# Keys of a pair copied by ScalarE alone, and one exponential moved behind a copy, in a multi-query attention kernel

## The chip, the cores and the metric

The kernel runs on one core of one Trainium2 chip. The metric is the device time of one execution in microseconds (us); the median of several runs is compared. Engines are named as the profile names them: PE is TensorE's matmuls and PEld its weight loads, DVE is VectorE, ACT is ScalarE, POOL is GpSimdE, SP is the engine that issues most DMAs.

## The reference

Multi-query attention with a residual over 64 batches of 128 tokens, width 512, 16 heads of 64; all heads share one set of keys and values. A null key and value, the first two rows of `cond`, stand ahead of the keys. Cut to what matters:

```python
xn = layernorm(x, g_in)
q = (xn @ Wq).reshape(b, n, H, DH).transpose(0, 2, 1, 3) * scale
kv = xn @ Wkv
k, v = (kv[..., :DH], kv[..., DH:])
k = jnp.concatenate([nk, k], axis=1); v = jnp.concatenate([nv, v], axis=1)
sim = jnp.einsum('bhid,bjd->bhij', q, k) + bias      # bias, causal mask, key mask
attn = jax.nn.softmax(sim, axis=-1)
out = jnp.einsum('bhij,bjd->bhid', attn, v)
out = out.transpose(0, 2, 1, 3).reshape(b, n, INNER) @ Wo
return x + layernorm(out, g_out)
```

The kernel subtracts the null key and the null value from all keys and values as they leave PSUM, so that the null column needs no matmul; the null value is added back to the attention's result.

## The kernel before

Batches are worked on in 32 pairs, and x is loaded and transposed in groups of four batches (two pairs). The program's order is written out by hand: each engine carries out its instructions in the order in which the code names them, and waits at an instruction whose operands are not ready. Pair d passes through `turn(d)` and then `body(d)`; `body_first` stands for pair 0, and `turn_end`, `body_end` and `body_last` for the last two pairs. So `body` runs 29 times, for d = 1 to 29.

A turn makes the scores of pair d on PE, adds the bias (DVE), takes maxima of the first half (DVE), takes the exponentials of the first half of the pair's first batch (`exps(a, 0)`, eight on ACT), multiplies the weights of the pair before by the values (PE, line 781, tile `po`) and has ACT add the null value and copy them out (line 800, tile `oT`).

A body then does four things at once for different pairs, interleaved by hand:

- Keys and values of the pair after next. `kv_pair` is eight matmuls (line 363) into the PSUM tile `pkv`: keys in partitions 0 to 63, values in 64 to 127. `kv_pair_out` copies them out: DVE takes the values (line 380, tile `vT`, 64x256), then the first two of the four blocks of 32 tokens of the keys (line 389, tile `kT`, 64x128), and ACT takes the other two blocks, one at a time (line 393, 64x64 each). In odd bodies `values_T` follows on DVE (line 401, tile `vb`), since then a group's values are complete. A DMA on SP doubles the keys (line 396).
- Queries of the pair after next, as the seven products of a Strassen scheme: `product(g, f, k, ...)` (line 515) is four matmuls of 256 columns. Products 1, 6, 7 and 4 add up in one PSUM tile `pa`, and between them `keep` (line 527) has ACT copy the intermediate sum to SBUF: `kp` after product 1, `ku` after product 6 and again after product 7. Product 7 adds to `pa` and so has to wait until the `ku` copy of product 6 has read it. Between product 6 and product 7, PE has product 5 into another tile, `pc` (four matmuls).
- The output projection of the pair before (`out_product`, line 868; tiles `pyX`, `pyY`, `pyw`) in the same scheme; `kyp` (line 882) is ACT's copy of its product 1. Its layer norm is two pairs late: statistics and the negated scaled mean `nmro` on DVE (line 919), the normalisation `yn` on ACT (line 926).
- The rest of the softmax: `exps(b, hf, lo, hi)` (line 683) is one ACT exponential per head row with an accumulated sum, `rinv` (line 701) on DVE, `scale` (line 705) on POOL, `blocks_T` (line 721) on DVE.

In an even body POOL also makes sums of tokens for the next group (`xS`, line 497), of which product 7 uses the third. GpSimd's power for the reciprocal root is line 281, tile `rstd`.

The exponentials of the pair's second batch, `exps(b, 0, ...)`, are dealt out between the copies: four ahead of `kyp` and the first `ku`, two behind them, `yn`, then the last two, then the `ku` of product 7.

Of the kernel before, what the change touches and what calls it, by code (L numbers as in the profile page):

```python
# [10 lines left out]
AF = mybir.ActivationFunctionType  # L11
ALU = mybir.AluOpType
# [5 lines left out]
def kernel(  # L18
# [59 lines left out]
    nc = tc.nc  # L78
# [19 lines left out]
    PLACE = 0, 1, 3, 2  # L98
# [47 lines left out]
    nkv = const.tile([P, 1], FP, name="nkv")  # L146
    nkv_neg = const.tile([P, 1], FP, name="nkv_neg")
# [201 lines left out]
    K_ROWS, V_ROWS = slice(0, DH), slice(DH, P)  # L349
# [25 lines left out]
    def kv_pair_out(m, pkv):  # L375
        g, t = divmod(m, GB)
        if t == 0:
            vTs[g] = hp.tile([P, GB, N], FP, tag="kv", name=f"vT_{g}", bufs=1)
        two = slice(t, t + 2)
        nc.vector.tensor_scalar(  # L380
            vTs[g][V_ROWS, two],
            pkv[V_ROWS].rearrange("p (t n) -> p t n", t=2),
            nkv[V_ROWS],
            None,
            ALU.subtract,
        )
        src = pkv[K_ROWS].rearrange("p (t i q) -> p t i q", t=2, i=NQ)
        out = kT[K_ROWS, :, two].rearrange("p i t q -> p t i q")
        nc.vector.tensor_scalar(
            out[:, :, 0:2], src[:, :, 0:2], nkv[K_ROWS], None, ALU.subtract  # L390
        )
        for i in (2, 3):
            nc.scalar.activation(
                out[:, :, i], src[:, :, PLACE[i]], AF.Identity, bias=nkv_neg[K_ROWS]
            )
        nc.sync.dma_start(out=kT[V_ROWS, :, two], in_=kT[K_ROWS, :, two])

# [280 lines left out]
    def exps(b, hf, lo=0, hi=R8):  # L678
        if hf == 0 and lo == 0:
            rsum[b] = small.tile([P, 2, R8], FP, tag="rsum", name=f"rsum_{b}")  # L680
        for k in range(lo, hi):
            row = S[b][:, k, WITH_NULL[hf]]
            nc.scalar.activation(  # L683
                row,
                row,
                AF.Exp,
                bias=nmax[b][:, hf, k : k + 1],
                accum_out=rsum[b][:, hf, k : k + 1],
            )
# [335 lines left out]
    def body_first():  # L1025
# [11 lines left out]
        for f in range(2):  # L1037
            product(g, f, 1, *rooms_a[f])
            keep_of(f, "p1")
        kv_pair_out(g * GB, pkv)  # L1040
        norm_apply(m)
        for f in range(2):
# [202 lines left out]
    def body(d):  # L1245

        a, b, p, l = 2 * d, 2 * d + 1, 2 * d - 2, 2 * d - 4
        g, h = d // 2 + 1, d % 2
        q, soft = g < NG, d > 0
        out, ln = 0 <= p <= P_LAST, 0 <= l <= P_LAST  # L1250
# [20 lines left out]
        if q:  # L1271
            kv_pair_out(g * GB + 2 * h, pkv)
            if h == 1:
                values_T(g)
# [28 lines left out]
            pair_residual(l)  # L1303
            store(l)
        if soft:
            exps(b, 0, 0, 4)
        if out:
            out_sum(p, 0)
        if sums:
# [7 lines left out]
            product(g, f0, 6, ps_q, "a", start=False)  # L1317
            keep("a", "u2")
        if soft:
            exps(b, 0, 4, 6)  # L1320
        if ln:
            pair_norm(l + 1, (ps_y, "Y"))
        if q:
# [166 lines left out]
    norm_stats(6)  # L1490
    null_negative()
    kv_pair_out(0, pkv)
    norm_stats(7)
    causal(1)
# [81 lines left out]
    for d in range(1, PAIRS - 2):  # L1576
        turn(d)
        body(d)
# [42 lines left out]
```

## Time and profile before

| what | value |
|---|---|
| median of 3 runs | 1035.4 us (1035.14 to 1035.87) |
| the profiled execution's own time | 1035.41 us |
| its span, first to last instruction | 1033.6 us |
| PE / PEld busy | 1021.9 us (99%) / 895.9 us (87%) |
| DVE / ACT / POOL busy | 805.6 / 689.1 / 744.8 us |
| granted TensorE clock, mean | 1.000 |

Times in the views are microseconds from the span's start. A row of the timeline gives start, length, engine, line, operation and tiles, the count of merged instructions, and in brackets the engine's idle time ahead and what ended it. A row of the waits gives who waited for whom, the total, how often, and the longest. The chain of work that ended last shows piece by piece (start, length, engine, tile, line) what each step was released by; "issue" in it is time without a wait that the profile shows. Buffer numbers are left out of names in the profile (`ku`, `pa`).

### The profile page before, as it was taken

What the parts mean: (1) busy time and instruction counts of PE and PEld (TensorE: products, weight loads), DVE (VectorE), ACT (ScalarE), POOL (GpSimd) and SP (SyncE); (2) the same over time, 40 slices, a digit from 0 to 9 for tenths busy, and PEclk for the clock granted to TensorE, in tenths of its full rate; (3) what the DMA queues carried; (4) which work ended last, traced back from release to release, by engine and by line L of the source; (5) the groups of instructions that cost most, each with busy time, mean ns of one, the idle gap of its engine ahead of it and who ended that gap; (6) DMA issues with size and microseconds to landing.
All of it is one profiled execution on the core that took longest, in us unless ns stands there. A gap on an engine that the chain in (4) does not pass through costs nothing.

```text
span 1033.6 us, 31331 instructions
## 1 busy us (share of the span) xinstructions
PE 1021.9 (99%) x12345; PEld 895.9 (87%) x12345; DVE 805.6 (78%) x1806; ACT 689.1 (67%) x2773; POOL 744.8 (72%) x579
## 2 busy tenths in 40 slices
PE   9999999999999999999999999999999999999997
PEld 8888888888888888888888888888888888888886
DVE  6877777877778877788777788777887777877697
ACT  4766667666677666686656776666776667856582
POOL 4997768686685857758677686766868678586676
PEclk9999999999999999999999999999999999999999
DMA  6414152141522315233152421415223151230211
GB/s 212 141 56 127 65 153 82 54 129 63 164 75 91 99 60 165 68 107 113 44 151 68 132 98 49 139 62 158 81 71 109 63 170 69 92 88 28 82 64 62
DMA packets 73835, 100.86 MB, mean 98 GB/s; under 512 B 32212, under 2 KB 36056, under 8 KB 71896
## 3 DMA queue, kind: packets, MB, share of 16 engines
q1 hardware_dynamic: 73392, 98.47, 31.0%
q8 instruction: 96, 1.57, 0.7%
q14 instruction: 51, 0.42, 0.1%
q10 hardware_dynamic: 296, 0.40, 0.1%
HBM read 63.19 MB, written 33.55 MB: 94 GB/s over the span
## 4 chain that ended last, share of the span: by engine, by line
PE 90%; ACT 4%; DVE 3%; issue 1%; POOL 1%; DMA 0%; POOLq 0%; DVEq 0%; ACTq 0%
PE pa L515 18%; PE pyX L868 17%; PE pyY L868 10%; PE pc L515 9%; PE po L781 7%; PE pkv L363 6%; PE pyw L868 5%; PE pl L581 4%; PE pq L450 3%; PE ps L652 3%; PE sc_X L652 2%; ACT s L683 2%; PE sc_Y L652 2%; PE py_s L868 1%; PE sc_a L652 1%
## 5 line engine op out<-in xcount | busy, mean ns | idle before, releaser
L683 ACT ACTIVATE s<-s,nmax 128x65 f32<-128x65 f32 (+1 forms) x1024 | 372.7, 368 | 62.5 <-DVE nmax L674 62.5
L705 POOL TENSOR_TENSOR s<-s,rinv 128x512 f32<-128x512 f32 (+1 forms) x132 | 190.6, 1445 | 152.2 <-DVE rinv L701 152.2
L617 POOL TENSOR_TENSOR s<-biasp,mneg 128x1552 f32<-128x1552 f32 (+1 forms) x65 | 206.1, 3173 | 51.1 <-DVE s L667 38.2
L683 ACT ACTIVATION_READ_ACCUMULATOR s<-s,nmax 128x1 f32 x1024 | 196.2, 192 | 0.0
L515 PE MATMUL pa<-xS,wq 128*128 128x256 f32 x472 | 123.8, 385 | 2.3 <-ACT ku L527 2.3
L533 ACT COPY qT<-pa 128x256 f32<-128x256 f32 x59 | 22.0, 372 | 153.5 <-PE pa L515 153.5
L674 DVE TENSOR_REDUCE nmax<-s 128x8 f32<-128x1032 f32 (+1 forms) x128 | 121.7, 951 | 0.1
L721 DVE STREAM_TRANSPOSE sb<-s 128x1536 f32<-128x1536 f32 (+1 forms) x68 | 113.5, 1672 | 2.0 <-POOL s L705 2.0
L868 PE MATMUL pyX<-wT,oT 128*128 128x256 f32 x464 | 109.7, 379 | 0.0
L868 PE MATMUL pyX<-wo,oT 128*128 128x256 f32 x464 | 109.7, 379 | 0.0
L515 PEld LDWEIGHTS pa<-xS,wq 128*128 128x128 f32 x472 | 85.1, 190 | 21.6 <-ACT ku L527 7.9
L868 PEld LDWEIGHTS pyX<-wo,oT 128*128 128x128 f32 x464 | 86.0, 190 | 10.5
L868 PEld LDWEIGHTS pyX<-wT,oT 128*128 128x128 f32 x464 | 85.9, 190 | 10.7
L848 POOL TENSOR_TENSOR oT<-oT 128x512 f32<-128x512 f32 x64 | 80.4, 1274 | 4.3 <-PE pyw L868 2.1
L781 PE MATMUL po<-sb,vr 32*64 32x256 f32 (+1 forms) x4064 | 81.0, 300 | 0.0
L781 PEld LDWEIGHTS po<-sb,vr 32*64 32x64 f32 x4064 | 70.9, 130 | 8.1 <-issue 5.7
L281 POOL TENSOR_TENSOR rstd<-rstd,nhalf 128x1 f32<-128x1 f32 x64 | 35.1, 555 | 57.0 <-DVE rstd L280 54.5
L536 DVE TENSOR_TENSOR qT<-pc,ku 128x256 f32<-128x256 f32 x118 | 48.5, 411 | 33.1 <-PE pc L515 18.9
L597 DVE TENSOR_TENSOR qT<-pl,kp 128x128 f32<-128x128 f32 x112 | 31.1, 277 | 55.5 <-PE pl L581 53.8
L800 ACT ACTIVATE oT<-po,nv 128x512 f32<-128x512 f32 (+1 forms) x127 | 73.7, 654 | 0.1
L363 PE MATMUL pkv<-xT,wkv 128*128 128x256 f32 x256 | 63.3, 391 | 0.0
L515 PE MATMUL pc<-xS,wS 128*128 128x256 f32 x236 | 60.6, 379 | 0.0
(187 smaller groups left out, 2402.6 us busy)
## 6 DMA issues: line engine op xcount, KB each, us to landing
res<-in_x_dram SPq DMA_DIRECT2D x64, 256.0 KB
x<-in_x_dram SPq DMA_DIRECT2D x63, 256.0 KB
out_dram<-y SPq DMA_DIRECT2D x63, 256.0 KB
xd<-xb SPq DMA_DIRECT2D x14, 1024.0 KB
xT<-xd SPq DMA_DIRECT2D x56, 256.0 KB
vr<-vd SPq DMA_DIRECT2D x64, 128.0 KB
kT<-kT SPq DMA_DIRECT2D x32, 64.0 KB
vd<-vb SPq DMA_DIRECT2D x32, 64.0 KB
```

Of the source, the lines that this page charges most:

```text
L363: nc.tensor.matmul(pkv, wkv[:, kc, :], xT[g][:, t : t + 2, kc, :], start=(kc == 0), stop=(kc == KC - 1),)
L515: nc.tensor.matmul(prod[tag], w[:, kc, f * P : (f + 1) * P], t[:, :, kc, :], start=(start and kc == 0), stop=(kc == HK - 1), skip_group_ch ...
L617: nc.gpsimd.tensor_tensor(S[b][:, :, keys], biasp[:, :, keys], mneg[:, t, keys] .unsqueeze(1) .broadcast_to([P, R8, keys.stop - keys.start ...
L652: nc.tensor.matmul(home[r][u * DH : (u + 1) * DH, f, :], qT[g, f, t // 2][rows, t % 2, hf, u], kT[rows, 0 : nk // Q, t, :], start=True, st ...
L674: nc.vector.tensor_reduce(nmax[b][:, hf], S[b][:, :, WITH_NULL[hf]], AX.X, ALU.max, negate=True)
L683: nc.scalar.activation(row, row, AF.Exp, bias=nmax[b][:, hf, k : k + 1], accum_out=rsum[b][:, hf, k : k + 1],)
L705: nc.gpsimd.tensor_tensor(sv, sv, rinvs[b, hf][:, lo:hi].unsqueeze(2).broadcast_to([P, hi - lo, sv.shape[2]]), ALU.mult,)
L721: nc.vector.transpose(sbs[b][:, :, lo:hi].rearrange("p j e q -> p e j q"), S[b][:, lo:hi, 1 : ROW - 1].rearrange("p e (j k) -> p e j k", k=Q),
L781: nc.tensor.matmul(po[s][rows, to : to + n], vr[g][quad, t, PLACE[j], :], sb[quad, slots, r * NF : (r + 1) * NF, :], start=(turn == 0), st ...
L800: nc.scalar.activation(to, src, AF.Identity, bias=nv2)
L848: eng.tensor_tensor(o, a, b, op)
L868: nc.tensor.matmul(prod[key], h[:, c, :], w[:, c, :], start=(start and c == 0), stop=(c == HC - 1), skip_group_check=not start,)
```

## The change

`kv_pair_out` no longer has DVE copy the first two key blocks; ACT copies all four, in three instructions (two blocks together, then one and one). DVE keeps the values alone. In `body`, the fourth exponential of `exps(b, 0, ...)` moves from ahead of `kyp` and the first `ku` to behind them.

```diff
@@ kv_pair_out
         src = pkv[K_ROWS].rearrange("p (t i q) -> p t i q", t=2, i=NQ)
         out = kT[K_ROWS, :, two].rearrange("p i t q -> p t i q")
-        nc.vector.tensor_scalar(
-            out[:, :, 0:2], src[:, :, 0:2], nkv[K_ROWS], None, ALU.subtract
-        )
-        for i in (2, 3):
+        for at, to, n in ((0, 0, 2), (3, 2, 1), (2, 3, 1)):
             nc.scalar.activation(
-                out[:, :, i], src[:, :, PLACE[i]], AF.Identity, bias=nkv_neg[K_ROWS]
+                out[:, :, to : to + n],
+                src[:, :, at : at + n],
+                AF.Identity,
+                bias=nkv_neg[K_ROWS],
             )
         nc.sync.dma_start(out=kT[V_ROWS, :, two], in_=kT[K_ROWS, :, two])
@@ body
         if soft:
-            exps(b, 0, 0, 4)
+            exps(b, 0, 0, 3)
@@ body
             product(g, f0, 6, ps_q, "a", start=False)
             keep("a", "u2")
         if soft:
-            exps(b, 0, 4, 6)
+            exps(b, 0, 3, 6)
```

The rows below are the built program's order, without times; rows with - stand before, rows with + after the change. On DVE, in the body of pair 3 (`pkv_1758` is its keys and values, `vT_1375` the group's values, `nmro` the negated means of the two late batches):

```order
 L908 TENSOR_SCALAR rstdo_1772<-mvo_1770 128x1
 L380 TENSOR_SCALAR vT_1375<-pkv_1758,nkv 64x256
-L389 TENSOR_SCALAR kT<-pkv_1758,nkv 64x2x2x32
 L401 STREAM_TRANSPOSE vb_1780<-vT_1375 64x512
 L919 TENSOR_SCALAR nmro_1790<-mvo_1567,rstdo_1569 128x1
```

The key copy is gone from DVE, and the transpose of the values and the two `nmro` follow the values' copy directly. On ACT, at the same place, from the last two copies of the attention's result (`oT`) to the first normalisation (`yn`):

```order
 L800 ACTIVATE oT_1749<-po_2_1670,nv_88 128x2x8x32
 L800 ACTIVATE oT_1749<-po_3_1671,nv_88 128x2x8x32
-L393 ACTIVATE kT<-pkv_1758,nkv_neg 64x64 x2
+L390 ACTIVATE kT<-pkv_1758,nkv_neg 64x2x2x32
+L390 ACTIVATE kT<-pkv_1758,nkv_neg 64x64 x2
 L527 COPY kp_1812<-pa_2_1_1809 128x256
 L926 ACTIVATE yn_1814<-y_1464,nmro_1790,rstdo_1569 128x512
```

ACT has one more instruction of 64 partitions by 128 elements ahead of the two that it had. On ACT, directly behind that (`s_1555` is the scores of the pair's second batch; the - and + rows of `kyp` and `ku` differ by buffer numbers alone):

```order
-L683 ACTIVATE s_1555,rsum_1827<-s_1555,nmax_1763 128x65 x4
-L882 COPY kyp_1839<-pyX_1_1834 128x256
-L527 COPY ku_1845<-pa_2_1_1809 128x256
-L683 ACTIVATE s_1555,rsum_1827<-s_1555,nmax_1763 128x65 x2
+L683 ACTIVATE s_1555,rsum_1827<-s_1555,nmax_1763 128x65 x3
+L882 COPY kyp_1838<-pyX_1_1833 128x256
+L527 COPY ku_1844<-pa_2_1_1809 128x256
+L683 ACTIVATE s_1555,rsum_1827<-s_1555,nmax_1763 128x65 x3
 L926 ACTIVATE yn_1849<-y_1576,nmro_1792,rstdo_1772 128x512
```

One exponential of the four ahead of `kyp` and `ku` now stands behind them. PE, POOL and SP have the same instructions in the same order as before.

## The prediction

> **What bounds the kernel now.** I read the page's first section, then who waits on PE and PEld, then one body of each parity row by row, then the chain through the odd one.
>
> ```profile
> PE 1021.9 (99%) x12345; PEld 895.9 (87%) x12345; DVE 805.6 (78%) x1806; ACT 689.1 (67%) x2773; POOL 744.8 (72%) x579
> ```
>
> PE is busy for 99% of the span; no other engine is above 78%. So the time is PE's, and the change, which leaves PE's instructions alone, can only pay where PE stands waiting. By the waits of the weight loads and, last row, of the matmuls:
>
> ```profile
> PEld pa L515 <- ACT ku L527: 7.9, 14, 0.6
> PEld pa L515 <- POOL rstd L281: 3.9, 13, 0.3
> PEld pa L515 <- POOL yS L848: 0.3, 1, 0.3
> ```
>
> ```profile
> PE pa L515 <- ACT ku L527: 2.3, 14, 0.2
> ```
>
> 14 times a load for `pa` waits 0.56 us for ACT's `ku`, and 13 + 1 times 0.3 us. I looked at where these stand: the first kind once in each odd body from 3 to 29, the second once in each even body from 2 to 28, always ahead of product 7 of the body's first column pair. Here are products 6, 5, 7 and the next PE work, first in an odd body, then in the even one behind it:
>
> ```profile
> 448.81 1.03 PE L515 MATMUL pa<-xS,wS 128*128 128x256 f32 x4
> 449.67 1.03 PE L515 MATMUL pc<-xS,wS 128*128 128x256 f32 x4
> 450.86 1.13 PE L515 MATMUL pa<-xS,wq 128*128 128x256 f32 x4 [0.16 <-ACT ku L527]
> 451.83 1.89 PE L868 MATMUL pyw<-wo,oT 128*128 128x256 f32 x8
> ```
>
> ```profile
> 480.46 1.03 PE L515 MATMUL pa<-xS,wS 128*128 128x256 f32 x4
> 481.33 1.03 PE L515 MATMUL pc<-xS,wS 128*128 128x256 f32 x4
> 482.27 1.10 PE L515 MATMUL pa<-xS,wq 128*128 128x256 f32 x4
> 483.21 1.03 PE L868 MATMUL pyw<-wo,oT 128*128 128x256 f32 x4
> ```
>
> Unhindered, four such matmuls take 0.86 us from start to start (448.81 to 449.67), so products 5 and 7 together should take 1.73. They take 451.83 - 449.67 = 2.16 in the odd body and 483.21 - 481.33 = 1.88 in the even one: **0.43 and 0.15 us lost**. The row shows 0.16 of idle only, since the modelled end of product 5 hides the rest. The weight loads give the same delay another way:
>
> ```profile
> 449.46 0.84 PEld L515 LDWEIGHTS pc<-xS,wS 128*128 128x128 f32 x4
> 450.86 0.73 PEld L515 LDWEIGHTS pa<-xS,wq 128*128 128x128 f32 x4 [0.56 <-ACT ku L527]
> ```
>
> ```profile
> 481.11 0.84 PEld L515 LDWEIGHTS pc<-xS,wS 128*128 128x128 f32 x4
> 482.24 0.73 PEld L515 LDWEIGHTS pa<-xS,wq 128*128 128x128 f32 x4 [0.29 <-POOL rstd L281]
> ```
>
> Product 7's first load should come 0.86 behind product 5's, at 450.32 and 481.97. It is 0.54 and 0.27 late and costs 0.43 and 0.15. So the first **0.11 us of lateness are free**, twice the same figure.
>
> What makes it late in the odd body is the chain that ended last:
>
> ```profile
> 446.20 0.04 DVE vT L380
> ...
> 446.72 0.35 DVE kT L389
> ...
> 447.09 0.71 DVE vb L401
> ...
> 447.83 0.23 DVE nmro L919
> ...
> 448.14 0.78 ACT yn L926
> 448.92 1.36 ACT s L683 x8
> 450.29 0.26 ACT kyp L882
> 450.54 0.28 ACT ku L527
> ...
> 450.86 1.13 PE pa L515 x4
> ```
>
> It runs through both things that the change touches: DVE's key copy (0.35 us) delays `nmro`, which delays `yn`; behind `yn` stand four exponentials (1.36 us with their accumulator reads), `kyp` and `ku`.
>
> **The change part by part.** *DVE loses line 389.* The values' copy ends at about 446.70; the next DVE row starts at 446.72 instead of 447.09, so `vb`, `nmro` and, if ACT is ready, `yn` come 0.35 earlier: `yn` at 447.79.
>
> *ACT gains one copy.* Rows needed:
>
> ```profile
> 447.15 0.51 ACT L393 ACTIVATE kT<-pkv,nkv_neg 64x64 f32<-64x64 f32 x2 [0.40 <-DVE kT L389]
> 447.56 0.36 ACT L527 COPY kp<-pa 128x256 f32<-128x256 f32 x1
> ...
> 450.44 0.36 ACT L527 COPY ku<-pa 128x256 f32<-128x256 f32 x1
> ```
>
> ```profile
> 478.80 0.51 ACT L393 ACTIVATE kT<-pkv,nkv_neg 64x64 f32<-64x64 f32 x2 [0.39 <-PE pa L515]
> ...
> 481.76 0.37 ACT L527 COPY ku<-pa 128x256 f32<-128x256 f32 x1
> ```
>
> ```profile
> L800 ACT ACTIVATE oT<-po,nv 128x512 f32<-128x512 f32 x116 | 69.2, 672 | 0.0
> ...
> L393 ACT ACTIVATE kT<-pkv,nkv_neg 64x64 f32<-64x64 f32 x64 | 16.3, 302 | 17.0 <-DVE kT L389 10.9 <-PE pa L515 6.1
> ```
>
> Both groups are the same function with a bias column, read from PSUM: 302 ns for 64 elements, 672 for 512. A straight line gives 355 ns for 128. Two 64-wide ones move the queue on by 447.56 - 447.15 = 0.41, 0.205 each, so neighbours overlap by 0.10, and the new copy moves it on by **0.26 us**. Bounds: 0.20 (the 64-wide one) and 0.57 (the 512-wide one). I take 0.26, near the lower end, as the row of 64 is the nearer one. [...]
>
> In the built program the first key copy waits for DVE's values' copy (446.70) where it waited for DVE's key copy (447.07). The hand-over took 0.08 (447.07 to 447.15), so ACT starts at 446.79 instead of 447.15, 0.36 earlier, and ends its key work at 446.79 + 0.26 + 0.41 = 447.46; `kp` takes 0.26 of queue, and ACT could start `yn` at 447.72. `nmro` allows 447.79. So the added copy is hidden behind `nmro`, with 0.07 to spare.
>
> *One exponential moves.* A quarter of 1.36 is 0.34. So `yn` 447.79, exponentials 448.57 to 449.59, `kyp` to 449.84, and `ku` could start there: 0.35 + 0.34 earlier. But now something else is late: product 6 itself.
>
> ```profile
> 462.67 1.03 PE L515 MATMUL pa<-xS,wq 128*128 128x256 f32 x4
> ```
>
> ```profile
> 463.78 0.37 ACT L527 COPY ku<-pa 128x256 f32<-128x256 f32 x1 [0.74 <-PE pa L515]
> ```
>
> An ACT that stands ready starts its copy 0.08 after the product's modelled end (463.70 to 463.78). Product 6 ends at 448.81 + 1.03 = 449.84, so `ku` starts at 449.92, ends at 450.28, and the load follows 0.06 later as before (450.80 to 450.86): 450.34, 0.02 late, within the free 0.11. **The 0.43 goes wholly.**
>
> *Even body.* ACT starts its keys 0.36 earlier (478.44), has 0.26 more to do (-0.10 from there on), and one exponential less (-0.34): `ku` could start at 481.32. Product 6 ends at 480.46 + 1.03 = 481.49, so `ku` starts at 481.57 and ends at 481.94; with 0.11 to the load as before (482.13 to 482.24), 482.05, 0.08 late: free. **The 0.15 goes too.** This takes the load there to wait for `ku`, whose end is 0.11 ahead of it, rather than for POOL's `rstd`, which product 7 does not read.
>
> *What is behind.* The moved exponential puts off the `ku` of product 7 by 0.34. In the odd body ACT reaches the first `ku` 0.52 earlier (449.92 for 450.44), so it is still ahead; in the even one only 0.19 earlier (481.57 for 481.76), so the second comes 0.15 later than here:
>
> ```profile
> 484.07 0.37 ACT L527 COPY ku<-pa 128x256 f32<-128x256 f32 x1
> ```
>
> ```profile
> 485.50 0.73 PEld L515 LDWEIGHTS pa<-xS,wq 128*128 128x128 f32 x4
> ```
>
> Product 4's load, which needs that copy, comes 1.06 behind its end now, and would still come 0.76 behind with the copy at 484.59 and the load 0.15 earlier. The keys' DMA leaves about when it did, and its keys are read two turns later. The one place where PE, now earlier, may meet DVE is product 5 of the odd body's second column pair, whose tile is free when DVE has read it:
>
> ```profile
> 456.45 0.42 DVE L536 TENSOR_TENSOR qT<-pc,ku 128x256 f32<-128x256 f32 x1
> ```
>
> ```profile
> 456.93 0.73 PEld L515 LDWEIGHTS pc<-xS,wS 128*128 128x128 f32 x4
> ```
>
> DVE works without a pause from `vT` to there and ends at 456.87, just 0.06 ahead of the load. DVE gains 0.35, PE 0.43, so the load comes 0.08 late. That is under 0.11: I cost it at nothing, and if the margin is missing there it costs up to 0.08 x 14 = 1.1 us.
>
> **Sum**, against the profiled execution (1035.41 us, span 1033.6): 14 x 0.43 + 14 x 0.15 = 6.0 + 2.1 = 8.1 us. 1035.4 - 8.1 = 1027.3; the median of the runs shown is the same 1035.4. Body 1 has no such wait, and the start and the last pairs I cost at nothing (PE has no wait on a key copy there).
>
> **The rivals.**
> - *Given back in the same body*, by DVE as above or by a like margin: 1.1 us, so 1028.4; with a second such place as costly, 1029.5. For it: DVE's unbroken row of work. Against: the margin of 0.11, seen twice.
> - *The even bodies stay.* The profile puts their wait down to POOL. If that is right, only 14 x 0.43 = 6.0 goes: 1029.4. Against: `ku` ends later (482.13) than anything of POOL that product 7 reads.
> - *Only the matmul's idle time goes.* 14 x 0.16 = 2.3 us, so 1033.1. For it: it is all that PE's own row shows as idle. Against: the spacing of 2.16 where 1.73 is due. [...]
> - *Slower: the key copy becomes ACT's bottleneck.* With c for its queue time, the path through ACT costs product 7 c - 0.50 in the odd body (446.79 + c + 0.41 + 0.26, then 0.78 + 1.02 + 0.25, 0.42 for `ku` and the hand-over, less 450.32 and 0.11) and about c - 0.53 in the even one. Today's loss of 0.58 a pair of bodies is reached at c = 0.81. At c = 1.0 the loss is 0.97, 14 x 0.39 = 5.5 us more: 1040.9. Against: 64 partitions by 128 elements would have to take longer than 128 by 512 do (0.57, at which only 14 x 0.11 = 1.5 us of the gain is lost: 1028.8).
> - *It doesn't free ACT at all*, the wait for DVE only changing its name and the added copy eating the moved exponential: 0.34 - 0.26 = 0.08 a body at most, 28 x 0.08 = 2.2, or nothing: 1033 to 1035.4. Against: DVE's own 0.35 in the chain is gone whatever ACT does.
>
> **How the numbers follow.** Forecast 1027.3 (1026.5 to 1028.2): 0.62. Given back: 0.14. Even bodies stay: 0.11. Matmul idle only or not freed: 0.07. Slower: 0.04. More than forecast: 0.02. The range holds the first three and the bound of 0.57 for the copy: 1026.3 to 1030.0, some 0.87, and the next case stands far off. A measurement of this kernel tells about 0.2% (2.1 us) from no change: faster 0.92 (the first three, the last and about half of the fourth), same 0.04, slower 0.04.
>
> **What the next profile would show.** Right: no PEld wait on `ku` ahead of product 7 in the first column pair, or under 0.1 us; products 5 and 7 start 1.73 apart from product 5 to `pyw` in both parities; `ku` waits for PE's product 6 there; `yn` starts 0.35 earlier after `vT`; odd and even bodies equally long. Wrong: a key copy much over 0.36 us; a new PEld wait for DVE's line 536 or `nmro` no earlier; an even body still 0.15 longer than the sum of its matmuls.

## The result, and the profile after

| | before | after |
|---|---|---|
| median of 6 runs | 1035.38 us (1035.14 to 1035.87) | 1029.51 us (1029.32 to 1029.80) |
| ratio after : before, 95% interval | | 0.9943 [0.9931, 0.9956] |
| profiled execution: own time, span | 1035.41, 1033.6 | 1029.77, 1027.9 |
| odd body, from `po` to `po` | 31.66 (body 1: 31.39) | 31.40 (body 1: 31.39) |
| even body | 31.39 | 31.23 |

The kernel is 5.9 us faster, 2.2 less than the 8.1 of the forecast. The body lengths in the last two rows say where. They come from the chain of work that ended last, in which each body is preceded by one long piece of PE work on the tile `po`. First the kernel before, then the changed one (start, length, engine, tile, line, merged instructions):

```profile
441.78 2.45 PE po L781 x123
473.44 2.45 PE po L781 x122
504.82 2.45 PE po L781 x123
```

```profile
439.50 2.45 PE po L781 x123
470.90 2.45 PE po L781 x123
502.13 2.45 PE po L781 x123
```

The odd body went from 473.44 - 441.78 = 31.66 to 31.40, the even one behind it from 31.38 to 31.23. These are the same in all bodies of a parity to 0.02, but for body 29, which is 31.22 after. So the even bodies gave 14 x 0.16 = 2.2 us, as forecast (0.15 each); the odd ones gave 13 x 0.255 and 0.43 in body 29, 3.7 us where 6.0 was forecast. Together that is about 6.0; the last pairs take 0.3 to 0.4 of it back (from the `po` behind body 29, at 977.79 and 971.72, to the end of the span: 55.8 before, 56.2 after). This stands in every run below that has all keys on ACT and in none that has some on DVE; why was not pursued.

The page's busy times after, then the first line of its chain by engine, before and after:

```profile
PE 1018.8 (99%) x12345; PEld 899.6 (88%) x12345; DVE 799.0 (78%) x1774; ACT 699.1 (68%) x2805; POOL 745.2 (72%) x579
```

```profile
PE 90%; ACT 4%; DVE 3%; issue 1%; POOL 1%; DMA 0%; POOLq 0%; DVEq 0%; ACTq 0%
```

```profile
PE 97%; DVE 1%; POOL 1%; issue 0%; POOLq 0%; DVEq 0%
```

DVE has 32 instructions less and ACT 32 more. PE is now 97% of the chain, 90% before: ACT, by which it ran ahead of each odd body's product 7, is gone from it. Of the weight loads' waits these are now the first, and none of product 7's (`pa`, line 515) on `ku` or `rstd` is left, where there were 7.9 and 3.9 us:

```profile
PEld sc_Y L652 <- issue: 10.1, 31, 0.3
PEld po L781 <- issue: 5.3, 31, 0.2
PEld pkv L363 <- DVE s L667: 4.8, 28, 0.2
```

The first column pair of the odd body, on PE, then its weight loads, then ACT:

```profile
446.53 1.03 PE L515 MATMUL pa<-xS,wS 128*128 128x256 f32 x4
447.39 1.03 PE L515 MATMUL pc<-xS,wS 128*128 128x256 f32 x4
448.25 1.03 PE L515 MATMUL pa<-xS,wq 128*128 128x256 f32 x4
449.12 1.24 PE L868 MATMUL pyw<-wo,oT 128*128 128x256 f32 x5
```

```profile
447.18 0.84 PEld L515 LDWEIGHTS pc<-xS,wS 128*128 128x128 f32 x4
448.04 0.84 PEld L515 LDWEIGHTS pa<-xS,wq 128*128 128x128 f32 x4
```

```profile
444.44 0.76 ACT L390 ACTIVATE kT<-pkv,nkv_neg 64x128 f32<-64x128 f32 x3
445.10 0.36 ACT L527 COPY kp<-pa 128x256 f32<-128x256 f32 x1
445.49 0.78 ACT L926 ACTIVATE yn<-y,nmro,rstdo 128x512 f32<-128x512 f32 x1
...
447.59 0.37 ACT L527 COPY ku<-pa 128x256 f32<-128x256 f32 x1
```

Products 5 and 7 take 449.12 - 447.39 = 1.73, their undisturbed time: the 0.43 is gone from this place entirely. `ku` now starts 1.06 behind product 6 (446.53), so it is that product's end it waits for, and it is done (447.96) before product 7's load is due (447.18 + 0.86). So what the odd body still has over the even one must stand elsewhere. It stands at product 5 of the second column pair, on PE, PEld and DVE:

```profile
453.24 1.03 PE L515 MATMUL pa<-xT,wq 128*128 128x256 f32 x4
454.11 0.38 PE L581 MATMUL pl<-xL,wq 128*128 128x128 f32 x2
454.40 1.13 PE L515 MATMUL pc<-xS,wS 128*128 128x256 f32 x4
455.37 1.24 PE L868 MATMUL pyY<-wT,yS 128*128 128x256 f32 x5
```

```profile
453.89 0.41 PEld L581 LDWEIGHTS pl<-xL,wq 128*128 128x128 f32 x2
454.40 0.73 PEld L515 LDWEIGHTS pc<-xS,wS 128*128 128x128 f32 x4
```

```profile
453.94 0.41 DVE L536 TENSOR_TENSOR qT<-pc,ku 128x256 f32<-128x256 f32 x1
```

DVE's line 536, which frees `pc`, ends at 454.35, and the load follows at 454.40. From there to `pyY` product 5 takes 0.97 instead of 0.86, and it starts 0.07 late behind the two `pl` matmuls (0.29 for 0.22): 0.18 us lost. No view of waits shows this one, since the load's row stands only 0.10 behind the end of the row ahead of it (453.89 + 0.41) and most of the delay hides in that modelled end.

Why DVE came so late shows in its own row, from the values' copy on. In the changed kernel:

```profile
443.92 0.49 DVE L380 TENSOR_SCALAR vT<-pkv,nkv 64x256 f32<-64x256 f32 x1 [0.54 <-PE pkv L363]
444.44 0.71 DVE L401 STREAM_TRANSPOSE vb<-vT 64x512 f32<-64x512 f32 x1
...
447.45 1.22 DVE L674 TENSOR_REDUCE nmax<-s 128x8 f32<-128x1032 f32 x1
448.70 0.29 DVE L597 TENSOR_TENSOR qT<-pl,kp 128x128 f32<-128x128 f32 x1
```

and the last two in the kernel before:

```profile
450.09 1.22 DVE L674 TENSOR_REDUCE nmax<-s 128x8 f32<-128x1032 f32 x1
451.23 0.28 DVE L597 TENSOR_TENSOR qT<-pl,kp 128x128 f32<-128x128 f32 x1
```

The 0.37 us of the key copy are gone ahead of `vb`. But line 597 now comes 1.25 us behind the start of line 674, where it came 1.14 behind before: it used to start 0.08 before that instruction's end and now starts after it (below this is called the hold of line 597). This is so in all 28 bodies from 2 to 29 of either kernel (1.24 or 1.25 after, 1.13 or 1.14 before). From the values' copy to line 536 DVE takes 10.02 us (443.92 to 453.94) after and 10.25 before (446.20 to 456.45): it gained 0.23 or 0.24, not the 0.35 that the forecast counted on.

### The profile page after: what moved, and what is told of

The parts are those of the page before. It is cut to its first block, busy times and chain, and to the rows that moved or that the text cites. A ratio compares the mean times of both kernels' runs of the same rounds, so it can differ in the third digit from the quotient of the medians.

```text
span 1027.9 us, 31287 instructions
## 1 busy us (share of the span) xinstructions
PE 1018.8 (99%) x12345; PEld 899.6 (88%) x12345; DVE 799.0 (78%) x1774; ACT 699.1 (68%) x2805; POOL 745.2 (72%) x579
## 3 DMA queue, kind: packets, MB, share of 16 engines
q8 instruction: 96, 1.57, 0.6%
## 4 chain that ended last, share of the span: by engine, by line
PE 97%; DVE 1%; POOL 1%; issue 0%; POOLq 0%; DVEq 0%
PE pa L515 20%; PE pyX L868 19%; PE pyY L868 10%; PE pc L515 10%; PE po L781 7%; PE pkv L363 6%; PE pyw L868 5%; PE pl L581 4%; PE pq L450 3%; PE ps L652 3%; PE sc_X L652 2%; PE sc_Y L652 2%; PE py_s L868 1%; PE sc_a L652 1%; PE sc_w L652 1%; PE busy L1453 1%
## 5 line engine op out<-in xcount | busy, mean ns | idle before, releaser
L515 PE MATMUL pa<-xS,wq 128*128 128x256 f32 x472 | 121.2, 379 | 0.0
L515 PEld LDWEIGHTS pa<-xS,wq 128*128 128x128 f32 x472 | 87.2, 190 | 11.1 <-issue 0.2
L527 ACT COPY ku<-pa 128x256 f32<-128x256 f32 x118 | 43.4, 368 | 28.3 <-PE pa L515 23.8
```

Source lines behind the costliest of these rows:

```text
L515: nc.tensor.matmul(prod[tag], w[:, kc, f * P : (f + 1) * P], t[:, :, kc, :], start=(start and kc == 0), stop=(kc == HK - 1), skip_group_ch ...
```

## The experiments

**The theory:** both edits do to product 7 what the forecast said, but in the odd bodies PE then runs into DVE's line 536, 0.18 us too early, for two reasons: there is no free margin at that place, and DVE lost 0.11 us of its gain to the hold of line 597. **Rivals:** the rest of the odd bodies' loss is the added key copy on ACT; or the two edits do not both matter; or the hold has another cause. Each kernel ran five times or more beside the kernel before on the same chip. All ten runs:

| run | median us | ratio to before, 95% interval | odd / even body |
|---|---|---|---|
| keys alone | 1030.09 | 0.9949 [0.9937, 0.9962] | 31.40 / 31.23 |
| exponential alone | 1032.67 | 0.9974 [0.9963, 0.9985] | 31.65 / 31.23 |
| values read from partition 0 | 1028.13 | 0.9933 [0.9919, 0.9946] | 31.27 / 31.23 |
| residual later | 1027.43 | 0.9924 [0.9912, 0.9936] | 31.23 / 31.23 |
| key copy made twice | 1030.54 | 0.9953 [0.9940, 0.9965] | 31.40 / 31.28 |
| before, keys first on DVE | 1036.90 | 1.0016 [1.0007, 1.0024] | 31.78 / 31.39 |
| keys alone, residual later | 1028.46 | 0.9935 [0.9921, 0.9948] | 31.29 / 31.23 |
| exponential alone, residual later | 1028.35 | 0.9932 [0.9919, 0.9944] | 31.35 / 31.23 |
| before, residual later | 1035.18 | 0.9999 [0.9990, 1.0008] | 31.66 / 31.39 |
| both cures | 1027.41 | 0.9925 [0.9911, 0.9938] | 31.23 / 31.23 |

The first four ran beside a kernel before of 1035.38 us, the next four beside 1035.20, the last two beside 1035.19.

### The keys alone

The changed kernel with the exponentials divided as before:

```diff
-            exps(b, 0, 0, 3)
+            exps(b, 0, 0, 4)
...
-            exps(b, 0, 3, 6)
+            exps(b, 0, 4, 6)
```

> The changed kernel with four exponentials again ahead of kyp and the first ku: the key part alone. Theory (PE waits for ScalarE's ku in the first column pair, and in odd bodies for VectorE's line 536 in the second): yn 0.35 us earlier, so product 7's load in the odd body about 0.29 late where it was 0.54 before the change and is on time after it: 0.43 lost there becomes about 0.18; VectorE gains 0.23 against PE's 0.25, so nothing more is lost in the second column pair. Even body: load about 0.17 late, 0.06 lost where 0.15 was. Gain 14 x (0.25 + 0.09) = 4.8 us: 1030.6. Rival (the moved exponential does the work, the key part only pays for it): near 1035.

Measured 1030.09: 0.6 us above the changed kernel and 5.3 below the one before. The loads of products 5 and 7 in the odd body:

```profile
447.18 0.84 PEld L515 LDWEIGHTS pc<-xS,wS 128*128 128x128 f32 x4
448.22 0.73 PEld L515 LDWEIGHTS pa<-xS,wq 128*128 128x128 f32 x4 [0.20 <-ACT ku L527]
```

Product 7's load is 0.18 behind its due 448.04, and from product 5 to `pyw` PE takes 1.79, 0.06 more than undisturbed. The expectation had 0.29 and 0.18 here: 0.29 was a slip, since 0.54 less DVE's 0.35 is 0.19. In the even bodies the load comes 0.11 late and nothing is lost, where 0.17 and 0.06 were expected. Yet the odd body is as long as in the changed kernel, 31.40: of the 0.18 lost there, 0.06 moved from line 536's place to this one and 0.12 stayed (the load of product 5 in the second column pair comes 0.45 behind the first of `pl`, 453.96 to 454.41, and 0.33 if nothing holds it). Body 1 is 0.2 longer (31.59). The keys carry most of the gain; behind them the moved exponential adds little, because in the odd bodies DVE has already set the end.

### The exponential alone

The kernel before with the two lines of `exps` as changed:

```diff
-            exps(b, 0, 0, 4)
+            exps(b, 0, 0, 3)
...
-            exps(b, 0, 4, 6)
+            exps(b, 0, 3, 6)
```

> The kernel before with the one exponential moved and the keys as they were: VectorE keeps its key copy. Theory: product 7's load comes about 0.34 us earlier in the odd body (0.43 lost becomes about 0.09), but VectorE has gained nothing, so the load of product 5 in the second column pair, which waits for line 536, comes about 0.34 late and loses what was won: odd body gains 0 to 0.05 us. Even body: the 0.15 goes, since VectorE has room there. 14 x 0.15 = 2.1, at most 2.8 us: 1032.6 to 1033.3. Rival (only ScalarE's path to ku matters): 14 x (0.34 + 0.15) = 6.9 us, 1028.5.

Measured 1032.67, 2.7 us faster, all of it in the even bodies and body 29. The odd ones stay at 31.65, though ACT's wait is down: products 5 and 7 take 1.83 (from product 5's load to `pyw`'s, 448.45 to 450.28), 0.10 lost where it was 0.43. Of the weight loads' waits:

```profile
PEld pc L515 <- DVE qT L536: 4.2, 21, 0.2
```

The load waits for line 536, here by name: 13 of the 21 are this load, once in each odd body from 3 to 27 (the other 8 are the load before it into `pc`, which costs 0.02). It comes 0.64 behind the first of `pl` (455.28 to 455.92), 0.31 late, and PE loses 0.30 there. What ACT gave at product 7, DVE took back at product 5 of the second column pair. The two edits alone give 5.3 + 2.7 = 8.0 us, together 5.9: the missing 2.1 is a place at which both end up.

### Values read from partition 0

Both causes are tried one at a time. First the hold: the values' copy takes all 128 partitions of its tile, so that DVE's read begins at partition 0, as line 597's does (it writes unused rows as well).

```diff
-            vTs[g][V_ROWS, two],
-            pkv[V_ROWS].rearrange("p (t n) -> p t n", t=2),
-            nkv[V_ROWS],
+            vTs[g][:, two],
+            pkv.rearrange("p (t n) -> p t n", t=2),
+            nkv,
```

> The changed kernel, but VectorE's copy of the values reads all 128 partitions of pkv from partition 0 on, in one instruction of the same 256 columns; the 64 rows more that it writes are read by nobody. Theory (after a PSUM read from partition 64, the next VectorE instruction that reads PSUM from partition 0, line 597, starts only when the maximum ahead of it has ended: 1.25 us from start to start where it was 1.13 with the key copy between them): the distance returns to 1.13, line 536 ends 0.12 earlier after vT, the load of product 5 in the second column pair of the odd body is 0.07 late instead of 0.19, and 0.05 to 0.07 is lost there instead of 0.175: 14 x 0.11 = 1.5 us less than the changed kernel, 1028.0. Rival (the 0.12 comes from what other engines do at that moment): distance stays 1.25 and the time 1029.5.

Measured 1028.13. On DVE, and the loads of the second column pair:

```profile
443.08 0.48 DVE L380 TENSOR_SCALAR vT<-pkv,nkv 128x256 f32<-128x256 f32 x1 [0.54 <-PE pkv L363]
...
446.60 1.22 DVE L674 TENSOR_REDUCE nmax<-s 128x8 f32<-128x1032 f32 x1
447.74 0.28 DVE L597 TENSOR_TENSOR qT<-pl,kp 128x128 f32<-128x128 f32 x1
```

```profile
453.05 0.41 PEld L581 LDWEIGHTS pl<-xL,wq 128*128 128x128 f32 x2
453.43 0.73 PEld L515 LDWEIGHTS pc<-xS,wS 128*128 128x128 f32 x4
```

1.14 again, with the instructions between the copy and line 597 unchanged. Product 5's load comes 0.38 behind the first of `pl` (0.51 in the changed kernel), and the odd body is 31.27. This is about what the prediction's DVE gain of 0.35 gives, with the margin missing.

### The residual later

Then DVE's work ahead of line 536: the residual of the late pair's second batch (`pair_residual(l + 1)`, line 932) and its store go behind the copies of the second column pair of queries. Some of the expectations below call it the next pair's residual; it is the same one.

```diff
-        if ln:
-            pair_residual(l + 1)
-            store(l + 1)
...
+        if ln:
+            pair_residual(l + 1)
+            store(l + 1)
```

> The changed kernel with VectorE's residual addition of the odd late batch (line 932, 0.6 us of its queue) and its store moved from ahead of to behind line 536 that frees the tile of product 5 in the second column pair. Theory (that wait is all that is left of the loss): line 536 ends 0.6 us earlier in the odd body, product 5's load is on time, odd bodies become as long as even ones (31.23 us), 14 x 0.17 = 2.4 us less than the changed kernel: 1027.1. Rival (the odd body's missing 0.17 us is lost elsewhere, or the moved addition comes late for the tile of pyY): 1029.5 or more.

Measured 1027.43, 2.1 us below the changed kernel. The same two loads, where nothing is late, then PE:

```profile
452.75 0.41 PEld L581 LDWEIGHTS pl<-xL,wq 128*128 128x128 f32 x2
453.08 0.73 PEld L515 LDWEIGHTS pc<-xS,wS 128*128 128x128 f32 x4
```

```profile
452.96 0.38 PE L581 MATMUL pl<-xL,wq 128*128 128x128 f32 x2
453.19 1.03 PE L515 MATMUL pc<-xS,wS 128*128 128x256 f32 x4
```

Undisturbed, the load stands 0.33 behind the first of `pl`. So it is 0.18 late in the changed kernel, which loses 0.18 a body there, and 0.05 in the run above, which loses 0.04: at this place all lateness is paid. Odd and even bodies are now equal.

### The key copy made twice

Is the key copy on ACT hidden? The copy of the first two blocks is made twice, to the same place.

```diff
-        for at, to, n in ((0, 0, 2), (3, 2, 1), (2, 3, 1)):
+        for at, to, n in ((0, 0, 2), (0, 0, 2), (3, 2, 1), (2, 3, 1)):
```

> The changed kernel with ScalarE's copy of the first two key blocks (64 x 128, 0.20 to 0.26 us of ScalarE's queue, 363 ns to its end) made twice, to the same place. Theory (the added key copy is hidden: the spare time in front of the reciprocal's product, and behind that the end of query product 6, take it up): 28 bodies x about 0.26 us more of ScalarE's work move the time by next to nothing, 1029.5 us, give or take 0.4. Rival (ScalarE's own row of work sets when query product 7 may load, so each such copy is paid for): 28 x 0.25 = 7 us, about 1036.5.

Measured 1030.54, 0.6 above the theory's upper end, 6 below the rival. In the even body ACT's `kp` starts 1.05 behind the first key copy (475.98 to 477.03), where it is 0.66 in the changed kernel: the repeated copy takes 0.39 of ACT's queue, more than the 0.26 of the expectation (why was not tried). Then:

```profile
479.00 0.36 ACT L882 COPY kyp<-pyX 128x256 f32<-128x256 f32 x1
479.25 0.38 ACT L527 COPY ku<-pa 128x256 f32<-128x256 f32 x1
```

`ku` follows `kyp` without a wait for product 6, which it has in the changed kernel (0.16 us there). Product 7's load comes 0.17 late (479.74, due at 478.71 + 0.86) and the even body pays 0.06; in the odd body it comes 0.11 late, which is free. So 28 x 0.39 = 10.9 us of ACT's time cost about 1 (a gain of 4.7 us in place of 5.9): one copy is hidden, a second just not, in the even bodies.

### Before, with the keys first on DVE

The hold in the kernel before, without any change of the work: DVE's key copy stands ahead of its values' copy, so that the last read of PSUM before line 597 begins at partition 64.

```diff
+        nc.vector.tensor_scalar(
+            out[:, :, 0:2], src[:, :, 0:2], nkv[K_ROWS], None, ALU.subtract
+        )
...
-        nc.vector.tensor_scalar(
-            out[:, :, 0:2], src[:, :, 0:2], nkv[K_ROWS], None, ALU.subtract
-        )
```

> The kernel before, with VectorE's key copy ahead of its values' copy; the same work. Theory (VectorE's read of PSUM on partitions 0 to 127 is held until the instruction ahead has ended when the last read of PSUM began at another partition; before, the key copy, which begins at partition 0, stood between): the span from the start of line 674 to the first copy of the row sums becomes 1.25 us in place of 1.13, VectorE reaches line 536 later by 0.12, and query product 5 of the odd bodies' second column pair pays for it: 14 x 0.12 = 1.6 us, about 1037.0. The copy of the other key blocks on ScalarE, which waits for VectorE's last copy either way, starts no earlier. Rival (the 0.12 us has another cause, such as ScalarE's own read of the same tile at the same time): 1.13 us and 1035.4.

Measured 1036.90, 1.7 us slower. On DVE:

```profile
450.43 1.22 DVE L674 TENSOR_REDUCE nmax<-s 128x8 f32<-128x1032 f32 x1
451.68 0.29 DVE L597 TENSOR_TENSOR qT<-pl,kp 128x128 f32<-128x128 f32 x1
```

1.25, and the odd bodies are 0.12 longer, the even ones not. Products 5 and 7 of the first column pair take 2.16 as before (450.00 to 452.16); the loads of the second column pair show where it is paid, at product 5:

```profile
456.94 0.41 PEld L581 LDWEIGHTS pl<-xL,wq 128*128 128x128 f32 x2
457.38 0.73 PEld L515 LDWEIGHTS pc<-xS,wS 128*128 128x128 f32 x4
```

Product 5's load comes 0.44 behind the first of `pl`, 0.33 before. So the order of two copies is enough to bring the hold, and it is paid where line 536 is late.

### Each edit alone, with the residual later

With DVE out of the way, what is each edit worth at product 7? The kernels are the two single edits, each with the move of the residual shown above.

> The key copies as changed, the exponentials split 4 and 2 as before, and the next pair's residual and its store behind the copies of the second column pair of queries, so that VectorE is out of that pair's way. Theory: what is left is query product 7 of the first column pair in the odd bodies, which the keys alone leave about 0.06 us late, so 14 x 0.06 = 0.8 us, and 0.2 in body 1, over the version with both edits and the residual late (1027.4): 1028.4. Rival (with VectorE out of the way the moved exponential is worth its forecast, 0.34 less the 0.11 that is free, in the odd bodies): 14 x 0.23 = 3.2 us, 1030.6.

> The moved exponential alone (the key copies as before), with the next pair's residual and its store behind the copies of the second column pair of queries. Theory (in the odd bodies the moved exponential took 0.34 of the 0.43 us lost ahead of product 7, and VectorE's line 536 took it back at product 5 of the second column pair): with VectorE out of the way 14 x 0.34 = 4.8 us of the odd bodies and 2.1 of the even ones go, 1035.4 - 6.9 = 1028.5. Rival (that pair's product 5 was not waiting for line 536): as the moved exponential alone, 1032.7.

Measured 1028.46 and 1028.35, both on the theory. The first loses 31.29 - 31.23 = 0.06 an odd body, at product 7. In the second the loads of products 5 and 7 are

```profile
446.61 0.84 PEld L515 LDWEIGHTS pc<-xS,wS 128*128 128x128 f32 x4
447.68 0.73 PEld L515 LDWEIGHTS pa<-xS,wq 128*128 128x128 f32 x4 [0.23 <-ACT ku L527]
```

447.68 - 446.61 - 0.86 = 0.21 late, for which it pays 0.10: the free 0.11 of the prediction, a third time (another 0.02 of the odd body's 0.12 goes at the `pc` load ahead of the second column pair). So either edit alone opens product 7 up to a tenth of a microsecond; alone and without the residual's move the exponential showed nothing of that in the odd bodies.

### The residual alone, and both cures

Is the late residual a gain of its own? And do the two cures act on one place?

> The kernel before, with only the next pair's residual and its store moved behind the copies of the second column pair of queries. Theory (that place became the limit of the odd bodies only once the change had let TensorE come earlier; before, line 536 ended 0.06 us ahead of the load that waits for it): no gain, 1035.3 us, give or take 0.4. Rival (the late residual is a gain of its own, whatever the rest does, since the version with the change and the late residual lies 2.1 us under the change): about 1033.2.

> The changed kernel with both cures of the second column pair's product 5 at once: the values copied from all 128 partitions of their tile (VectorE's read begins at partition 0), and the next pair's residual and store behind the copies of the second column pair. Theory (both act on the one place, VectorE's line 536 against product 5's load, and with the residual late nothing is left to win there): as the late residual alone, 1027.4 us, give or take 0.3. Rival (the two gains over the change, 1.4 and 2.1 us, come from different places and add up): about 1026.0.

Measured 1035.18 beside 1035.19, and 1027.41. The late residual gives nothing without the change, and the values' wider read gives nothing on top of it. It is one place, and it became a limit only through the change.

## Why the prediction was right, and where its sum was not

- *DVE loses line 389: 0.35 us.* Right as far as it was followed: `yn` starts 1.57 behind the values' copy (443.92 to 445.49), 1.94 before.
- *ACT's added copy, 0.26 of queue, hidden behind `nmro`.* Right, in the odd bodies, for which it was said. It takes 363 ns where about 355 were forecast, and the three copies hold ACT for 0.66 us (444.44 to 445.10), 0.67 forecast:

```profile
L390 ACT ACTIVATE kT<-pkv,nkv_neg 64x64 f32<-64x64 f32 x64 | 15.9, 298 | 0.0
...
L390 ACT ACTIVATE kT<-pkv,nkv_neg 64x128 f32<-64x128 f32 x32 | 11.6, 363 | 4.6 <-DVE vT L380 4.5
```

- *`ku` is then bound by product 6, and product 7's 0.43 goes wholly.* Right: 1.73 from product 5 to `pyw`. The run with the keys alone shows that the keys without the exponential would have left 0.06.
- *Even bodies: the 0.15 goes too, and the wait put down to POOL was ACT's.* Right, 0.16 each. In the run with the exponential alone and the residual later POOL's `rstd` starts 0.16 ahead of product 5's load in the even body as it did before (477.79 and 477.95; 480.95 and 481.11), yet product 7's load comes 0.91 behind that load (478.86) in place of 1.13. So the rival by which the even bodies stay (1029.4) gives the time measured by luck, and its mechanism is refuted. So are "the matmul's idle time alone", the rival by which ACT is not freed, and the slower case: the key copy would have had to take 0.81 us.
- *Product 5 of the second column pair: "the load comes 0.08 late. That is under 0.11: I cost it at nothing".* **This is the term that was mis-sized**, put at nothing, and the place was the right one. The load is 0.18 late, of which about 0.08 is as worked out and about 0.11 is DVE's gain lost to the hold of line 597 (0.24 instead of 0.35). And the margin of 0.11 does not exist here. It costs 13 x 0.18 = 2.3 us, about what the sum was off by (2.2), and keeps odd and even bodies from being equally long. This is the rival "given back in the same body", by one place at twice its price. Body 29, in which DVE takes no statistics of x (no row of line 270) and so reaches line 536 in time, kept the whole 0.43. The sign that the prediction named, a new wait for line 536, came, but in the spacing of the loads and not in the list of waits. The 1029.5 lies outside the 1026.5 to 1028.2 of the case given 0.62, and inside the whole range only because the rivals had widened it. With DVE moved out of the way the time is 1027.43, against the forecast of 1027.3.

The margin was carried from one place to another without its reason. At product 7 of the first column pair an undisturbed load starts 0.21 before its matmul (448.04 and 448.25 in the changed kernel). Behind the two `pl` matmuls of 128 columns, which PE takes 0.11 apart (452.96 to 453.19 for the two), the lead is down to 0.11 (453.08 for the load in the undisturbed run, 453.19 for its matmul), and a load that starts together with its matmul cost 0.10 within the product at both places (0.97 from its start to the next PE work: 450.86 to 451.83 before, 454.40 to 455.37 after). So what is free is the lead less 0.10: 0.11 there, nothing here. That the short matmuls are what uses up the lead is read from these rows; no run changed them.

## What to carry to other kernels

When a wait is taken away, PE arrives earlier at what stands behind it (here, with 0.43 us gone at product 7, 0.18 us too early for DVE's line 536): list the next places where it meets each engine, with the spare time of each, and charge a place fully unless its own rows show the slack, which here was 0.11 at one place and nothing at another. Two edits that aim at one wait may be worth less together (5.9 us here) than the sum of their single gains (5.3 + 2.7) because they end at the same next limit; a run of each alone shows it. And an engine from which an instruction is removed may gain less than that instruction's time: DVE gave up a copy of 0.35 us here and gained 0.24, since line 597 came 0.11 later behind the instruction ahead of it.

## What the runs showed of the hardware that was not expected

When DVE started line 597 went with what DVE had read before it. Line 597 reads PSUM from partition 0; with the last PSUM read at partition 64 it came 1.25 us after the start of the 1.22 us instruction ahead of it (the changed kernel, and the kernel before with its two copies exchanged), with it at partition 0 1.14 us (the kernel before, and the changed one with the values read from partition 0). So an overlap of about 0.11 us is lost, once in each of the bodies 2 to 29 of the changed kernel. The copy's output and its column of null values begin at partition 64 or 0 together with its read, and no run parts them; nor does a run show what holds the instruction.
